# Finishing a batch between the sums of the next: the last feed-forward of a two-layer decoder

## The chip, the cores and the metric

The kernel runs on one core of one Trainium2 chip. A core has a matmul engine (TensorE, PE in the profile, its weight loads PEld), a vector engine (VectorE, DVE), an activation engine (ScalarE, ACT), a general engine (GpSimd, POOL) and a queue for transfers (SyncE, SP). Each engine works through its own list of instructions in order and waits on semaphores for the others. The metric is device time in microseconds (us) of one execution.

## The reference, cut to what matters

The reference is a decoder of two layers with layer norms behind each of six stages, on x of shape 4 x 512 x 512 (four batches of 512 rows). Only the last stage is touched, the second feed-forward with weights packed to four bits:

```python
def _L1_ffn_ref(x, gate_up_packed, gate_up_scales, down_packed, down_scales):
    ...
    w_gu = _dequant_fp4(gate_up_packed, gate_up_scales, GROUP_SIZE)
    w_down = _dequant_fp4(down_packed, down_scales, GROUP_SIZE)
    gate_up = jnp.einsum('bsh,oh->bso', x, w_gu)
    gate, up = (gate_up[..., :I], gate_up[..., I:])
    h = jax.nn.silu(gate) * up
    y = jnp.einsum('bsi,hi->bsh', h, w_down)
    rms = jnp.sqrt(jnp.mean(y * y, axis=-1, keepdims=True) + EPS)
    return y / rms
...
x = _layernorm(x + _L1_ffn_ref(x, ...), axis=-1)
```

I is 1408 and a group of scales spans 128 inputs, so each output of the first product is a sum of four groups, each with a scale of its own.

## The kernel before, in words

The six stages are named A to F, and each runs batch by batch (A0 to A3, and so on to F0 to F3). Each batch of a stage is a Python generator; the function `lanes` keeps at most two alive and steps them in turn. A generator that says "next" lets the following batch begin, so the end of one batch is traced between the steps of the next one. A scheduling layer (Tile) then puts every engine's instructions in order. It keeps the program's dependences and hands out buffers; `tc.issue_after(ins)` adds an edge that puts the instructions of its block behind `ins` on the same engine. Within a generator a `Pipe` delays work by steps: `pipe.later(n, fn)` calls `fn` at the n-th `tick` from now.

The stage in question is `l1_ffn(b)`, F0 to F3. A batch has 11 units (128 of the 1408 inner columns each), a unit has two halves u (0 is gate, 1 is up) and each half four groups g. This makes 88 groups a batch, one a step:

- Two matmuls of 128x512 (L1106, `fg<-fxh,gu` and `fg<-fxl,gu`) fill one PSUM bank with the group's product. A step later `scaled` multiplies by the group's scale and adds. Group 0 of each half is copied by ScalarE (L1064), group 3 of the gate too (L1067); the five others of the unit are sums on VectorE (L1070, `fg<-fg,gs,fg`), 220 in all. GpSimd adds the gate's two parts (L1074).
- ScalarE applies silu (L1078), VectorE multiplies by up (L1082), ScalarE rounds the product to a high part (L1087) and GpSimd takes the low part (L1088).
- `down` multiplies the unit's result into four accumulators, one for each tile of 128 rows: three matmuls for each (L1097, `facc<-...`), spread over eight steps, so twelve a unit. An accumulator holds a PSUM bank from the batch's first unit to its last use.

PSUM has eight banks: four hold a batch's accumulators, and the others pass the groups' products on.

When the eleventh unit's `down` is through, the batch is finished: ScalarE squares each accumulator and sums it along the row (L1116, four times). VectorE takes the mean (L1119, fm), its reciprocal root in eleven small operations (L162, L163 and three times L170 to L172, all 128x4), adds accumulator times root to the residual x for each of the four tiles (L1123) and takes the statistics of the layer norm (L176, L177). A second reciprocal root follows (L185, then again L162 to L172, on ln), the four tiles are normed (L200) and stored. While that goes on for batch b, the groups of batch b+1 are already running on all engines. I call this stretch a handover; there are three (F0 to F1, F1 to F2, F2 to F3). Batch F3 is finished alone.

At the start of a batch, x is transposed by TensorE (L213, `fx<-ident,x`, 16 transposes).

Of the kernel before, what the change touches and what calls it, by code (L numbers as in the profile page):

```python
# [2 lines left out]

# [1 line left out]

# [9 lines left out]
I32 = mybir.dt.int32  # L15
U8 = mybir.dt.uint8
AF = mybir.ActivationFunctionType
ALU = mybir.AluOpType
# [3 lines left out]
B, S, D = 4, 512, 512  # L22
P = 128
NT = 4
MAGIC = 12582912.0
RSQRT_SEED = float(0x5F3759DF)
# [15 lines left out]
class Pipe:  # L42


    def __init__(self):
        self.todo = []
# [21 lines left out]
class Net:  # L68
    def __init__(self, ctx, tc, args):
        self.tc = tc  # L70
        self.nc = tc.nc
        self.a = args
        self.n = 0
        pool = lambda name, **kw: ctx.enter_context(tc.tile_pool(name=name, **kw))
        self.const = pool("const", bufs=1)
        self.op = pool("op", bufs=O_BUFS)
        self.tp = pool("tp", bufs=T_BUFS)
        self.xp = pool("xp", bufs=X_BUFS)
        self.wp_ = pool("wp", bufs=W_BUFS)
        self.small = pool("small", bufs=4)  # L80
        self.psum = pool("psum", bufs=8, space=PSUM)
        nc = self.nc
        tc.keep_in_program_order(nc.scalar.preload_act_table_set(LOG_EXP))
        self.ident = self.c("ident", [P, P])
        make_identity(nc, self.ident)
        self.ident16 = self.c("ident16", [P, P], BF16)
        nc.vector.tensor_copy(self.ident16, self.ident)
        self.ones = self.c("ones", [P, P])
        nc.gpsimd.memset(self.ones, 1.0)
        scratch = lambda name, shape: nc.dram_tensor(name, shape, F32, kind="Internal").ap()  # L90
        self.had_scratch = scratch("had_scratch", (2, NT, 2048, P))
        self.xd = [args["x"]] + [scratch(f"x{i}", (B, S, D)) for i in range(1, 6)] + [args["out"]]
        self.bg, self.table = {}, None
        self.gu, self.dn = {}, []
        self.pre = {}
        self.w1 = {}
        self.mean, self.scale = {}, {}
        self.tern = {name: {} for name in self.TERNARY}
# [69 lines left out]
    def newton(self, ve, y, t):  # L168
        nc = self.nc
        nc.vector.tensor_tensor(t, y, y, ALU.mult)  # L170
        nc.vector.scalar_tensor_tensor(t, t, -0.5, ve, ALU.mult, ALU.mult)
        nc.vector.scalar_tensor_tensor(y, t, 1.5, y, ALU.add, ALU.mult)  # L172

    def ln_stats(self, y, i, ln):
        nc = self.nc
        nc.vector.bn_stats(ln[:, 8:14], y)  # L176
        nc.vector.bn_aggr(ln[:, 2 * i : 2 * i + 2], ln[:, 8:14])  # L177

    def ln_tile(self):
        return self.s("ln", 32, 3)  # L180
# [867 lines left out]
    def l1_ffn(self, b):  # L1048
        nc = self.nc
        pipe = Pipe()  # L1050
        x = self.load_x(5, b)
        yield
        yield
        xT = []
        yield from self.feature_major(pipe, x, "fx", xT)
        yield from pipe.drain()
        acc, y, hs = [], {}, {}

        def scaled(i, u, g, ps):

            s = self.gs[:, (i * 2 + u) * 4 + g : (i * 2 + u) * 4 + g + 1]
            if g == 0:
                y[u] = self.t("fg")
                nc.scalar.activation(y[u], ps, AF.Copy, scale=s)  # L1064
            elif g == 3 and u == 0:
                y2 = self.t("fg2")
                nc.scalar.activation(y2, ps, AF.Copy, scale=s)  # L1067
                y[u, 2] = y2
            else:
                nc.vector.scalar_tensor_tensor(y[u], ps, s, y[u], ALU.mult, ALU.add)  # L1070
            if g == 3:
                o = y.pop(u)
                if (u, 2) in y:
                    nc.gpsimd.tensor_tensor(o, o, y.pop((u, 2)), ALU.add)  # L1074
                pipe.later(F_ACT, *((up, i, o) if u else (gate, o)))

        def gate(o):
            nc.scalar.activation(o, o, AF.Silu)  # L1078
            y["gate"] = o

        def up(i, o):
            nc.vector.tensor_tensor(o, o, y.pop("gate"), ALU.mult)  # L1082
            pipe.later(F_PAIR, pair, i, o)

        def pair(i, o):
            hi, lo = self.t("fhh", F32R), self.t("fhl", F32R)
            nc.scalar.copy(hi, o)  # L1087
            nc.gpsimd.tensor_tensor(lo, o, hi.bitcast(F32), ALU.subtract)  # L1088
            for t in range(NT):
                pipe.later(F_DOWN + 2 * t, down, i, t, (hi, lo))  # L1090

        def down(i, t, h):
            if len(acc) <= t:
                acc.append(self.pb("facc"))
            c = slice(t * P, (t + 1) * P)
            for n, (l, r) in enumerate(((0, 0), (0, 1), (1, 0))):
                nc.tensor.matmul(acc[t], h[l][:, c], self.dn[i][r], start=i == 0 and n == 0, stop=i == 10 and n == 2)  # L1097

        for i in range(11):
            self.need("F", lambda: len(self.dn) > min(10, i + 1))  # L1100
            for u in range(2):
                for g in range(4):
                    pipe.tick()
                    ps = self.pa("fg")
                    for n in range(2):
                        nc.tensor.matmul(ps, self.gu[i, u][:, g * P : (g + 1) * P], xT[g][n], start=n == 0, stop=n == 1)  # L1106
                    pipe.later(F_SCALED, scaled, i, u, g, ps)
                    yield
        yield "next"
        x = self.load_x(5, b)  # L1110
        yield from pipe.drain()
        fm = self.s("fm", 24, 2)
        ss, ve = fm[:, 0:4], fm[:, 4:8]
        for i in range(NT):
            sq = self.t("fsq")
            nc.scalar.activation(sq, acc[i], AF.Square, accum_out=ss[:, i : i + 1])  # L1116
            if i % 2:
                yield
        nc.vector.tensor_scalar(ve, ss, 1.0 / 512.0, 1e-6, ALU.mult, ALU.add)  # L1119
        r = self.rsqrt(ve, fm[:, 8:20])  # L1120
        ln = self.ln_tile()
        for i in range(NT):
            nc.vector.scalar_tensor_tensor(x[i], acc[i], r[:, i : i + 1], x[i], ALU.mult, ALU.add)  # L1123
            self.ln_stats(x[i], i, ln)
            if i % 2:
                yield
        self.finish(pipe, x, ln, 5, b)
        yield from pipe.drain()
# [124 lines left out]
```

## Time and profile before

| | us |
|---|---|
| median of three runs (1626.9 to 1636.79) | 1629.89 |
| the profiled execution, its own time | 1630.29 |
| its span, first to last instruction | 1628.6 |

| engine | busy us | share of the span | instructions |
|---|---|---|---|
| PE | 1532.3 | 94% | 8215 |
| DVE | 1247.6 | 77% | 2684 |
| ACT | 1010.6 | 62% | 2177 |
| POOL | 665.9 | 41% | 672 |

| line, engine, what | count | busy us | mean ns |
|---|---|---|---|
| L1070 DVE, sums of the groups | 220 | 162.4 | 745 |
| L1106 PE, `fg<-fxh,gu` | 352 | 143.7 | 408 |
| L1106 PE, `fg<-fxl,gu` | 352 | 138.8 | 394 |
| L1074 POOL, adding the gate's parts | 44 | 61.1 | 1388 |
| L1064 ACT, copies of group 0 | 88 | 60.4 | 686 |
| L1097 PE, `facc<-p4h,fhh` (one of three) | 176 | 71.2 | 406 |

A row of the timeline or of a group gives start and duration, engine, line, operation and `out<-in`; what stands in brackets is the idle time of the engine before it and what ended that. A busy PE isn't PE at its peak, since the ends of matmuls are modelled and overlap: the distance between the starts of matmuls says more. In rows by stretch, x is the number of instructions, and PEclk the clock that TensorE was granted, as a share of full speed. Stage F takes the last 350 us, from the first L1106 at 1280.0 us on.

### The profile page before, as it was taken

What the parts mean: (1) busy time and instruction counts of PE and PEld (TensorE: products, weight loads), DVE (VectorE), ACT (ScalarE), POOL (GpSimd) and SP (SyncE); (2) the same over time, 40 slices, a digit from 0 to 9 for tenths busy, and PEclk for the clock granted to TensorE, in tenths of its full rate; (3) what the DMA queues carried; (4) which work ended last, traced back from release to release, by engine and by line L of the source; (5) the groups of instructions that cost most, each with busy time, mean ns of one, the idle gap of its engine ahead of it and who ended that gap; (6) DMA issues with size and microseconds to landing.
All of it is one profiled execution on the core that took longest, in us unless ns stands there. A gap on an engine that the chain in (4) does not pass through costs nothing.

```text
span 1628.6 us, 25543 instructions
## 1 busy us (share of the span) xinstructions
PE 1532.3 (94%) x8215; PEld 1100.0 (68%) x8246; DVE 1247.6 (77%) x2684; ACT 1010.6 (62%) x2177; POOL 665.9 (41%) x672
## 2 busy tenths in 40 slices
PE   7999999999999999899999999999998889999995
PEld 5888786444544664476777767777676766687774
DVE  6476589999875788977575766657779898979795
ACT  4333336988777887787796756967543445454542
POOL 6663563555535204422334243342333244333332
PEclk9999999999999999999999999999999999999998
DMA  7143344455124734861523334232446331111000
GB/s 241 35 149 123 110 149 137 146 172 174 59 75 132 222 116 136 250 188 61 145 60 77 79 90 117 60 86 68 155 155 196 128 113 53 43 37 52 1 26 26
DMA packets 127812, 180.76 MB, mean 111 GB/s; under 512 B 16560, under 2 KB 51376, under 8 KB 127680
## 3 DMA queue, kind: packets, MB, share of 16 engines
q1 hardware_dynamic: 123552, 170.69, 33.7%
q0 software_dynamic: 4128, 8.46, 2.1%
q8 instruction: 65, 1.06, 0.3%
q14 instruction: 67, 0.55, 0.1%
HBM read 111.98 MB, written 41.94 MB: 95 GB/s over the span
## 4 chain that ended last, share of the span: by engine, by line
PE 61%; DVE 17%; ACT 9%; issue 5%; DMA 4%; POOL 3%; SPq 1%; DVEq 0%; ACTq 0%; POOLq 0%
PE fg L1106 7%; PE facc L1097 6%; PE dT L883 3%; PE bo L458 2%; ACT de L873 2%; PE dn L701 2%; PE bT L213 2%; DVE x L200 2%; PE pu L649 2%; PE bs L486 2%; DVE bsm L434 2%; PE pg L647 2%; PE do L903 2%; DVE fg L1070 2%; PE dq L150 2%
## 5 line engine op out<-in xcount | busy, mean ns | idle before, releaser
L1070 DVE SCALAR_TENSOR_TENSOR fg<-fg,gs,fg 128x512 f32<-128x512 f32 x220 | 162.4, 745 | 35.4 <-PE fg L1106 15.2
L869 DVE CUSTOM_DVE_ANT_0 de<-ds,negm,thr 128x128 f32<-128x128 f32 (+3 forms) x256 | 126.4, 546 | 34.3 <-PE ds L858 31.2
L1106 PE MATMUL fg<-fxh,gu 128*128 128x512 f32 x352 | 143.7, 408 | 8.0 <-DVE fg L1070 5.0
L873 ACT ACTIVATE de<-de,dm 128x128 f32<-128x128 f32 (+3 forms) x256 | 143.1, 563 | 12.4 <-DVE dm L869 11.9
L1106 PE MATMUL fg<-fxl,gu 128*128 128x512 f32 x352 | 138.8, 394 | 0.0
L442 POOL TENSOR_SCALAR be<-be,bsm 128x512 f32<-128x512 f32 x128 | 95.8, 761 | 104.5 <-DVE bsm L440 72.8
L624 POOL TENSOR_TENSOR hl<-g,hh 128x512 fp32r<-128x512 f32 x64 | 83.9, 1318 | 113.3 <-ACT hh L623 98.7
L1074 POOL TENSOR_TENSOR fg<-fg,fg 128x512 f32<-128x512 f32 x44 | 61.1, 1388 | 127.1 <-ACT fg L1067 74.5
L436 ACT ACTIVATE be<-bs,bsm 128x512 f32<-128x512 f32 x128 | 87.3, 690 | 31.3 <-DVE bsm L434 29.6
L800 POOL TENSOR_TENSOR dql<-dqf,dqh 128x512 fp32r<-128x512 f32 x32 | 41.3, 1290 | 155.3 <-ACT dqh L799 121.0
L883 PE MATMUL dT<-ident,de 128*128 128x128 f32 x640 | 89.6, 278 | 7.6 <-ACT de L873 5.8
L1106 PEld LDWEIGHTS fg<-fxh,gu 128*128 128x128 f32 x352 | 66.9, 190 | 38.4 <-DVE fg L1070 14.8
L883 PEld LDWEIGHTS dT<-ident,de 128*128 128x128 f32 x640 | 71.7, 141 | 25.3 <-ACT de L873 13.6
L1064 ACT ACTIVATE fg<-fg,gs 128x512 f32<-128x512 f32 x88 | 60.4, 686 | 39.2 <-PE fg L1106 38.6
L434 DVE TENSOR_REDUCE bsm<-bs 128x1 f32<-128x512 f32 x128 | 83.3, 672 | 0.0
L1097 PE MATMUL facc<-p4h,fhh 128*128 128x512 f32 x176 | 71.2, 406 | 8.9 <-DVE fg L1070 6.2
L458 PE MATMUL bo<-bpT,cT 128*64 128x512 f32 x256 | 76.9, 618 | 2.1 <-ACT bpT L449 1.2
L213 PEld LDWEIGHTS bT<-ident,be 128*128 128x128 f32 x512 | 55.0, 141 | 34.6 <-issue 10.3
L213 PE MATMUL bT<-ident,be 128*128 128x128 f32 x512 | 73.2, 281 | 4.4 <-POOL be L442 2.1
L1067 ACT ACTIVATE fg<-fg,gs 128x512 f32<-128x512 f32 x44 | 30.3, 688 | 73.4 <-PE fg L1106 73.4
L312 POOL TENSOR_TENSOR z<-z,rope_cos 128x512 f32<-128x512 f32 x32 | 45.7, 1438 | 73.0 <-DVE zs L310 66.0
L1106 PEld LDWEIGHTS fg<-fxl,gu 128*128 128x128 f32 x352 | 66.8, 190 | 11.9
(332 smaller groups left out, 4693.3 us busy)
## 6 DMA issues: line engine op xcount, KB each, us to landing
x<-x SPq DMA_DIRECT2D x176, 256.0 KB, 3.1
had_scratch<-hw SPq DMA_DIRECT2D x64, 256.0 KB, 2.4
z<-had_scratch SPq DMA_DIRECT2D x64, 256.0 KB, 5.8
stk<-dqh SPq DMA_DIRECT2D x192, 64.0 KB, 2.0
tw<-in_wg_t SPq DMA_DIRECT2D x32, 256.0 KB, 3.8
tw<-in_wu_t SPq DMA_DIRECT2D x32, 256.0 KB, 3.6
tw<-in_wd_t SPq DMA_DIRECT2D x32, 256.0 KB, 2.9
p<-in_gu_p SPq DMA_DIRECT2D x22, 256.0 KB, 2.7
```

What stands on the lines that cost most here:

```text
L213: self.nc.tensor.transpose(pt[:, i * P : (i + 1) * P], srcs[i][:, j * P : (j + 1) * P], self.ident)
L434: nc.vector.tensor_reduce(sm[:, h : h + 1], ps, AX.X, ALU.max, negate=True)
L436: nc.scalar.activation(e, ps, AF.Exp, bias=sm[:, h : h + 1], accum_out=sm[:, 2 + h : 3 + h])
L442: nc.gpsimd.tensor_scalar(es[h][i], es[h][i], sm[:, 4 + h : 5 + h], 1.0, ALU.mult, ALU.mult)
L458: nc.tensor.matmul(po[0][h * 64 : h * 64 + 64, :], cT[j][:, c : c + 64], pTs[h], start=j == 0, stop=j == NT - 1)
L624: nc.gpsimd.tensor_tensor(lo, g, hi.bitcast(F32), ALU.subtract)
L869: nc.vector.tensor_tensor_reduce(es[i], ps, self.negm[:, 384 - P * i :], -1.0, self.thr[:, i : i + 1], ALU.add, ALU.min, n4[:, i : i + 1])
L873: nc.scalar.activation(es[i], es[i], AF.Exp, bias=n4[:, i : i + 1], scale=-1.0, accum_out=den[:, hh * 4 + i : hh * 4 + i + 1])
L883: nc.tensor.transpose(pt[:, o + (i - j) * P : o + (i - j + 1) * P], es[i][:, j * P : (j + 1) * P], self.ident)
L1070: nc.vector.scalar_tensor_tensor(y[u], ps, s, y[u], ALU.mult, ALU.add)
L1097: nc.tensor.matmul(acc[t], h[l][:, c], self.dn[i][r], start=i == 0 and n == 0, stop=i == 10 and n == 2)
L1106: nc.tensor.matmul(ps, self.gu[i, u][:, g * P : (g + 1) * P], xT[g][n], start=n == 0, stop=n == 1)
```

## The change

Three things change for batches F0 to F2; the end of F3 stays as it is.

1. As soon as an accumulator has had its last matmul (`i == 10`), one step later, ScalarE copies it from PSUM to SBUF (`release`, a tile `fy` from the large pool), and all that follows reads the copy. The bank is free after the copy.
2. The squares on ScalarE and all of the finish on VectorE are cut into pieces, and `between` issues each piece alone: it waits for a step (up to four while the piece before is not yet followed by a sum), and puts the piece behind the engine's latest group operation (`self.emitted`) by an edge. `ahead` then puts the engine's next group operation behind the piece by another edge. The pieces on VectorE are: the mean; the root's first two operations; three times a Newton step of three operations; for each tile its L1123 and then its statistics; the variance plus epsilon; the second root in the same four pieces; four norms, each followed by its store.
3. `newton` and `ln_stats` return their last instruction, and the tile `ln` is taken earlier.

```diff
+    def between(self, engine, *ops):
+
+        yield
+        for _ in range(3):
+            if engine in self.piece:
+                yield
+        with self.tc.issue_after(self.emitted[engine].ins):
+            for op in ops:
+                self.piece[engine] = op()
+
+    def ahead(self, engine):
+
+        p = self.piece.pop(engine, None)
+        return self.tc.issue_after(p.ins) if p else nullcontext()
+
+    def rsqrt_spread(self, ve, s):
+
+        nc = self.nc
+        sh, y, t = s[:, 0:4], s[:, 4:8], s[:, 8:12]
+        yield from self.between(
+            "DVE",
+            lambda: nc.vector.tensor_scalar(sh.bitcast(I32), ve.bitcast(I32), 1, None, ALU.logical_shift_right),
+            lambda: nc.vector.tensor_scalar(y.bitcast(I32), sh.bitcast(I32), -1.0, RSQRT_SEED, ALU.mult, ALU.add),
+        )
+        for _ in range(3):
+            yield from self.between("DVE", lambda: self.newton(ve, y, t))
+        return y
...
             else:
-                nc.vector.scalar_tensor_tensor(y[u], ps, s, y[u], ALU.mult, ALU.add)
+                with self.ahead("DVE"):
+                    self.emitted["DVE"] = nc.vector.scalar_tensor_tensor(y[u], ps, s, y[u], ALU.mult, ALU.add)
...
+            if i == 10 and b + 1 < B:
+                pipe.later(1, release, t)
+
+        def release(t):
+
+            f = self.o("fy")
+            nc.scalar.copy(f, acc[t])
+            acc[t] = f
...
+        if b + 1 < B:
+            for i in range(NT):
+                sq = self.t("fsq")
+                yield
+                yield from self.between("ACT", lambda: nc.scalar.activation(sq, acc[i], AF.Square, accum_out=ss[:, i : i + 1]))
+            yield
+            yield from self.between("DVE", lambda: nc.vector.tensor_scalar(ve, ss, 1.0 / 512.0, 1e-6, ALU.mult, ALU.add))
+            r = yield from self.rsqrt_spread(ve, fm[:, 8:20])
+            for i in range(NT):
+                yield from self.between("DVE", lambda: nc.vector.scalar_tensor_tensor(x[i], acc[i], r[:, i : i + 1], x[i], ALU.mult, ALU.add))
+                yield from self.between("DVE", lambda: self.ln_stats(x[i], i, ln))
+            v2 = ln[:, 16:20]
+            yield from self.between("DVE", lambda: nc.vector.tensor_scalar(v2, ln[:, 0:8].rearrange("p (i two) -> p i two", two=2)[:, :, 1], 1e-5, None, ALU.add))
+            yield from self.rsqrt_spread(v2, ln[:, 20:32])
+            for i in range(NT):
+                yield from self.between("DVE", lambda: nc.vector.tensor_scalar(x[i], x[i], ln[:, 2 * i : 2 * i + 1], ln[:, 24 + i : 25 + i], ALU.subtract, ALU.mult))
+                nc.sync.dma_start(self.xd[6][b, i * P : (i + 1) * P, :], x[i])
+            return
```

The two copies on ScalarE in `scaled` (L1064 and L1067) are wrapped in `ahead("ACT")` and kept in `self.emitted["ACT"]` in the same way.

More of the change, by code (lines that the diff above doesn't have):

```diff
@@ L1 @@
 import math
-from contextlib import ExitStack
+from contextlib import ExitStack, nullcontext
 import numpy as np
@@ L92, in __init__ @@
         self.xd = [args["x"]] + [scratch(f"x{i}", (B, S, D)) for i in range(1, 6)] + [args["out"]]
-        self.bg, self.table = {}, None
+        self.bg, self.table, self.emitted, self.piece = {}, None, {}, {}
         self.gu, self.dn = {}, []
@@ L171, in newton @@
         nc.vector.scalar_tensor_tensor(t, t, -0.5, ve, ALU.mult, ALU.mult)
-        nc.vector.scalar_tensor_tensor(y, t, 1.5, y, ALU.add, ALU.mult)
+        return nc.vector.scalar_tensor_tensor(y, t, 1.5, y, ALU.add, ALU.mult)
+    def between(self, engine, *ops):
[20 more added lines that the diff above has]
+        return y
     def ln_stats(self, y, i, ln):
@@ L176, in ln_stats @@
         nc.vector.bn_stats(ln[:, 8:14], y)
-        nc.vector.bn_aggr(ln[:, 2 * i : 2 * i + 2], ln[:, 8:14])
+        return nc.vector.bn_aggr(ln[:, 2 * i : 2 * i + 2], ln[:, 8:14])
     def ln_tile(self):
@@ L1063, in scaled @@
                 y[u] = self.t("fg")
-                nc.scalar.activation(y[u], ps, AF.Copy, scale=s)
+                with self.ahead("ACT"):
+                    self.emitted["ACT"] = nc.scalar.activation(y[u], ps, AF.Copy, scale=s)
             elif g == 3 and u == 0:
                 y2 = self.t("fg2")
-                nc.scalar.activation(y2, ps, AF.Copy, scale=s)
+                with self.ahead("ACT"):
+                    self.emitted["ACT"] = nc.scalar.activation(y2, ps, AF.Copy, scale=s)
                 y[u, 2] = y2
             else:
-                nc.vector.scalar_tensor_tensor(y[u], ps, s, y[u], ALU.mult, ALU.add)
+                with self.ahead("DVE"):
+                    self.emitted["DVE"] = nc.vector.scalar_tensor_tensor(y[u], ps, s, y[u], ALU.mult, ALU.add)
             if g == 3:
@@ L1113, in l1_ffn @@
         ss, ve = fm[:, 0:4], fm[:, 4:8]
+        ln = self.ln_tile()
+        if b + 1 < B:
[16 more added lines that the diff above has]
+            return
         for i in range(NT):
@@ L1120, in l1_ffn @@
         r = self.rsqrt(ve, fm[:, 8:20])
-        ln = self.ln_tile()
         for i in range(NT):
```

## The prediction

> **What bounds the kernel now.** I read the page first, then busy time by stretch over the last feed-forward (1280 us to the end), then the timeline of VectorE, GpSimd and TensorE through one handover of a batch, and the chain of waits there. The change touches only this stage: in the built order of both kernels every engine's instructions are the same until batch F0 has finished its matmuls.
>
> Busy time by stretch, batch F1 handing over to F2 and the quiet part after it:
>
> ```profile
> core 0: us, PE busy (x) PEld busy (x) DVE busy (x) ACT busy (x) POOL busy (x), PEclk, DMA share, GB/s
> 1440.00:1460.00 20.00, 20.00 (x98) 16.68 (x97) 14.05 (x20) 9.93 (x16) 5.14 (x4) 1.00 0.16 53
> 1460.00:1480.00 20.00, 17.96 (x70) 13.61 (x69) 17.40 (x35) 10.02 (x21) 7.70 (x6) 0.91 0.00 0
> 1480.00:1500.00 20.00, 18.95 (x80) 14.11 (x79) 19.56 (x38) 10.03 (x16) 8.47 (x6) 1.00 0.08 28
> 1500.00:1520.00 20.00, 20.00 (x89) 16.54 (x89) 15.60 (x22) 9.29 (x15) 8.07 (x7) 1.00 0.23 79
> ```
>
> Outside the handover TensorE is the limit: 89 matmuls in 20 us, VectorE busy 15.6. In the handover it starts only 70 and 80, and VectorE is full (19.56 of 20). The timeline of VectorE and GpSimd there shows why it is so full:
>
> ```profile
> 1465.86 0.16 DVE L1119 TENSOR_SCALAR fm<-fm 128x4 f32<-128x4 f32 x1
> 1466.05 0.17 DVE L162 TENSOR_SCALAR fm<-fm 128x4 int32<-128x4 int32 x1
> 1466.11 1.30 POOL L1074 TENSOR_TENSOR fg<-fg,fg 128x512 f32<-128x512 f32 x1 [3.10 <-DVE fm L1119]
> 1466.26 1.18 DVE L163 TENSOR_SCALAR fm<-fm 128x4 int32<-128x4 int32 x1
> ...
> 1467.37 1.27 POOL L1088 TENSOR_TENSOR fhl<-fg,fhh 128x512 fp32r<-128x512 f32 x1
> ...
> 1467.47 1.18 DVE L170 TENSOR_TENSOR fm<-fm 128x4 f32<-128x4 f32 x1
> 1468.69 0.16 DVE L171 SCALAR_TENSOR_TENSOR fm<-fm 128x4 f32<-128x4 f32 x1
> 1468.77 0.75 DVE L1070 SCALAR_TENSOR_TENSOR fg<-fg,gs,fg 128x512 f32<-128x512 f32 x1
> 1469.44 0.15 DVE L172 SCALAR_TENSOR_TENSOR fm<-fm 128x4 f32<-128x4 f32 x1
> 1469.57 0.50 PE L1097 MATMUL facc<-p4h,fhh 128*128 128x512 f32 x1 [1.92 <-DVE fg L1070]
> ```
>
> A 128x4 operation of 0.17 us takes 1.18 us twice: each time it ends within 0.03 us of the end of a GpSimd operation (1467.41, 1468.64). I call that a port wait. The sums (L1070), which read PSUM, never show it (220 of them, at most 0.754 us). Meanwhile TensorE stands still for 1.92 us for want of a sum. The chain of waits at the end of the same handover:
>
> ```profile
> 1496.19 2.88 DVE x L200 x4
> 1499.07 0.67 DVE fg L1070
> 1499.74 0.04 issue
> 1499.79 1.20 PE fg L1106 x4
> ```
>
> The four norms stand in one lump ahead of a sum that TensorE waits for. So in the handover VectorE is the bound, and the banks between it and TensorE are its only slack.
>
> **What a handover costs now.** In the TensorE timeline the first transposes (L213) of F2 start at 1446.36, those of F3 at 1524.86: a period of 78.5 us. Its work is 176 matmuls of L1106 and 132 of L1097; forty in a row start in 9.07 us (1454.74 to 1463.81), 0.2268 us each, so 69.9 us, and 16 transposes at some 0.1 us make 71.5. Lost: 7.0 us. F2 to F3 repeats it to 0.1 us. F0 to F1 has the same stalls, but without the slow matmuls (0.43 us apart from 1470.4 to 1473.4, clock 0.91): 1 us less, 6.0. All three: 20.0 us, the most that this change can bring.
>
> **VectorE's account before.** From the first of the chain (1465.86) to the first sum behind the norms (1499.0) are 33.1 us, of which 1.0 idle (0.73 and 0.30) and 6.1 port waits, each an operation's time less its undisturbed time (1.01, 1.01, 1.09, 1.01, 0.55, 0.50 and 0.97 in the norms). Ten GpSimd operations fall into it: 0.61 us of wait for each. In this stretch TensorE passes 103 matmuls, 23.4 us at its pace. Excess 33.1 - 23.4 = 9.7 us; 7.0 were lost, so the banks swallowed 2.7.
>
> **The change, part by part.**
>
> *The pieces move.* In the built order the first piece came after the sum of group 106 (groups of two L1106 matmuls, numbered from F0's first; eight a unit), in the run of nine groups (104 to 112) that have no L1097 matmuls between them, where VectorE (five sums and a product, 4.3 us) is slower than TensorE (eight groups, 3.6 us) even without pieces. Now it comes after group 117, and one piece stands between any two sums until group 151. TensorE's share of that stretch is 119 matmuls, 27.0 us, against 23.4: this is the gain.
>
> *VectorE's work in it.* 22 sums at 0.67 us (start to start, 1468.77 to 1469.44) are 14.7; four products L1082 at 0.58, 2.3; 24 small operations, 14 at 0.19 and 10 (the last ahead of a sum) at 0.08, 3.5; four L1123 at 0.65, four L176 at 0.60, four L177 at 0.13, 5.5; four norms at 0.45 (L200 takes 0.525 at least, less overlap), 1.8. Together 27.8 us.
>
> *Port waits.* GpSimd's work goes by units: two operations a unit, 34 groups are 4.25 units, so 8.5 operations at 0.61, 5.2 us. New is that L1123 (L1163 after the change) reads fy from SBUF, not facc from PSUM. No row shows it; the nearest is L1082, two SBUF inputs, median 0.683 and at most 1.151 (it waits), against L1123 with PSUM, 0.717 to 0.751 (it never does). GpSimd is busy 41% of the time, the rest of an operation is 0.65 us on average: 0.27 each, 1.1 for four. I take 6.3 us. Ends: none (0) and every GpSimd operation hitting for its whole 1.30 us (11.1).
>
> The Trainium skill's page "SBUF — State Buffer", section "Who interferes with whom", speaks against this edit: a VectorE instruction with two SBUF inputs contends with a GpSimd instruction that reads SBUF, and whichever came second stands still for the whole of the other. The rows above agree for L170 and L1082. With all four caught at their whole length, the rule's worst, they would cost 5.2 us and not 1.1, 4.1 more a handover, and the sum would be 1635.8 us.
>
> *Sum of a handover.* 27.8 + 6.3 - 27.0 = 7.1 us of excess, less the same 2.7 of slack: 4.4 us lost. Gain 2.6 in F1 to F2 and F2 to F3, 1.6 in F0 to F1: 6.8 us.
>
> *ScalarE's copies.* Twelve of 128x512 out of PSUM (four a handover, the last batch has none); the nearest row is the cast L139 fxh<-fx, 0.59 us, so 2.4 us a handover. ScalarE is busy 10.0 of 20 us in both stretches and takes them in its gaps. Uncovered, each would push the L1064 copy queued behind it, and with it a bank, by up to 0.59 us; that is within the slack of four banks. In return the four accumulator banks are free some 14 us sooner (about 1464 against 1477.8), so the run of nine groups finds eight banks. The copies and the SBUF source leave L1116 at its 0.59 us.
>
> *Edges.* The squares stand between ScalarE's copies now, the fourth after group 115; VectorE's first piece, after group 117, comes 1.6 us of TensorE's time later, about when the square is done: at most 0.3 us. Behind it stands the sum of group 118. No instruction is added on VectorE or GpSimd, none removed. On SP the last store of a batch falls behind one x load; no one waits for the store. F3's own ending is as before, so a gain in any handover reaches the end whole.
>
> The Trainium skill's page "TensorE: Matmul & The Clock Gate", section "What's actually happening", has the slow clock come after an idle window of about 3.4 us. Here the 0.43 us cadence follows a standstill of 1.92 us, and at 1390.2 an equal standstill has none behind it. By the page no slow clock should be there to remove; by the trace it is 1 us in two handovers of three, inside the measured 7.0. By the page the gain would be 2 us smaller, 1625.5 us.
>
> **The sum.** The profiled execution took 1630.3 us (span 1628.6), 0.4 over the median of 1629.9. 1630.3 - 6.8 = 1623.5 us.
>
> **Rivals.**
> 1. *The forecast*, a small gain: port waits of 4 to 9 us a handover. At 4 the loss is 2.1, gains 4.9, 4.9 and 3.9, 1616.6 us; at 9 the loss is 7.1, 1631.6 us. Chance 0.74.
> 2. *All is hidden.* With port waits under 2 us nothing is lost and all 20.0 us come back: 1610.3 us. For it: VectorE has 9 us idle in the quiet 1425 to 1457. Against: ten GpSimd operations in a handover, seven of which hit. Chance 0.11.
> 3. *Slower by the port.* Pieces between all sums, and L1123 with two SBUF inputs, let nearly every GpSimd operation stop VectorE. From port waits of 8.9 us on (where the loss passes 7.0) the change loses; at 11.1 and 1 us idle the loss is 10.2, and 3.2 + 3.2 + 4.2 make 1640.9 us. For it: an alternation of 0.67 us sums with short all-SBUF pieces leaves no gap as long as 1.3 us. Against: the same alternation stood in the chain of 1486 to 1495, with 0.5 to 1.0 us a hit. Chance 0.15.
>
> **How the numbers follow.** The measurement tells about 1% (16.3 us) from no change; the three runs before lie 9.9 us apart. Most of the forecast is inside 1%, and so is nearly all of the third case; only the second, and a little of the first, go past 1613.6. Faster by over 1%: 0.11; within: 0.87; slower by over 1%: 0.02. The range runs from between the first and second cases to just past port waits of 9 us: 1613 to 1634.
>
> **What would show it.** Right: the period of F2 to F3 (first transposes to first transposes) falls from 78.5 to some 76 us; the 1.92 us standstill and the clock of 0.91 are gone; no lump of four norms in the chain; port waits of 4 to 9 us a handover, some now in L1163; VectorE still full between groups 117 and 151. Wrong: the period at 72 (port waits vanished, or more slack than 2.7 us), or over 78.5 (waits above 9 us, or a piece that waits for ScalarE's fourth square).

## The result, and the profile after

The change makes the kernel slower by a quarter of a per cent: 1635.06 us against 1630.39, medians of 22 runs each, ratio 1.0025 (95% interval 1.0014 to 1.0035). The forecast was 1623.5 us.

The profiled execution has a span of 1634.7 us, 6.1 more than before. Part of that is not the change: up to the first sum of F0 the two programs are the same, and this execution is 2.5 us later there (1287.4 against 1284.9). From there on it loses 3.7 us, all of it in the three columns that hold a handover. I measure from the first sum (L1070, L1101 after the change) of one batch to that of the next:

| us between first sums | F0 to F1 | F1 to F2 | F2 to F3 | first sum of F3 to the end |
|---|---|---|---|---|
| before | 89.5 | 77.2 | 78.5 | 98.4 |
| after | 89.5 | 78.6 | 79.3 | 100.0 |

The handover of F0 to F1 lies behind the first sum of F1 and so in the second column, that of F1 to F2 in the third, that of F2 to F3 in the last. The third column is called the period below.

Busy time by stretch, kernel after, F1 handing over to F2 (columns as in the prediction's table of stretches):

```profile
1460.00:1480.00 20.00, 20.00 (x89) 16.40 (x88) 15.96 (x26) 14.29 (x28) 7.78 (x6) 1.00 0.00 0
1480.00:1500.00 20.00, 16.77 (x71) 12.62 (x70) 19.04 (x39) 7.96 (x13) 6.24 (x5) 1.00 0.00 1
1500.00:1520.00 20.00, 17.65 (x76) 13.49 (x75) 16.52 (x30) 7.74 (x13) 7.28 (x6) 1.00 0.32 105
```

The first of the three was 70 matmuls before and is now full (89): the pieces are out of the run of nine groups, and the standstill of 1.92 us at its end is gone. But the next two start 71 and 76, and in the last VectorE is busy only 16.5 of 20 us. TensorE waits there for something that isn't VectorE's work. The chain of waits names it (start, duration, engine, tile, line):

```profile
1489.32 0.25 DVE fg L1113
...
1490.02 0.62 ACT fhh L1118
...
1490.77 1.69 POOL fhl L1119
1492.46 1.24 POOL fg L1105
1493.70 0.02 issue
1493.72 0.63 ACT fg L1109
1494.35 0.59 ACT fg L1093
1494.93 0.04 issue
1494.98 0.73 PE fg L1145 x2
```

A product on VectorE (L1113) is late. ScalarE's cast of it (L1118) waits; GpSimd's low part (L1119) waits for the cast; GpSimd's add (L1105), of the *next* unit, whose last input (a sum) was there at 1490.64, stands behind the low part until 1492.42; the silu (L1109) waits for that add; ScalarE's copy of the next group 0 (L1093) stands behind the silu; and TensorE has no bank until it is done. (The low part takes 1.69 us where most take 1.30. It starts while a sum into x, L1163, is running on VectorE; I take the 0.39 us for a port wait in the other direction, which is argued.) ScalarE's timeline of the same time, with the idle time before each in brackets:

```profile
1490.00 0.62 ACT L1118 CAST fhh<-fg 128x512 fp32r<-128x512 f32 x1 [0.75 <-DVE ln L205]
1493.72 0.63 ACT L1109 ACTIVATE fg<-fg 128x512 f32<-128x512 f32 x1 [3.09 <-POOL fg L1105]
1494.26 0.67 ACT L1093 ACTIVATE fg<-fg,gs 128x512 f32<-128x512 f32 x1
1496.91 0.69 ACT L1097 ACTIVATE fg<-fg,gs 128x512 f32<-128x512 f32 x1 [1.98 <-PE fg L1145]
1497.89 0.69 ACT L1093 ACTIVATE fg<-fg,gs 128x512 f32<-128x512 f32 x1 [0.29 <-PE fg L1145]
1498.47 0.61 ACT L1118 CAST fhh<-fg 128x512 fp32r<-128x512 f32 x1
```

The chain comes once a unit (the next two adds stand 2.8 and 1.6 us behind their last input), and from the second time on it feeds itself: the next product is ready at 1496.09, but its cast starts only at 1498.47, behind ScalarE's copies (L1097, L1093), which had waited for the delayed TensorE. Standstills of TensorE behind the copy end at 1495.0, 1503.1 and 1511.0 (2.6, 1.3 and 1.8 us from start to start, where 0.23 is usual; together 5.1 us beyond that, of which a little may be matmuls missing from the trace). One more, of 1.4 us, ends at 1486.0 with a late sum. F0 to F1 has the same four to 0.3 us. The waits of this handover, longest in total, show the same pairs:

```profile
POOL fhl L1119 <- ACT fhh L1118: 21.9, 5, 6.0
...
ACT fg L1109 <- POOL fg L1105: 10.5, 4, 3.1
PEld fg L1145 <- ACT fg L1093: 6.5, 5, 2.7
```

Before the change the last of these pairs took 0.7 us there, and GpSimd waited 6.6 us for the cast. What made the chain is in the built order, which was at hand before the result. ScalarE's instructions over groups 116 to 144 (units 14 to 18, counted from F0's first), g the copies by group, "cast" L1087 or L1118 and "silu" L1078 or L1109:

```
before    g116 cast silu g120 g123 g124 silu cast g128 g131 g132 cast g136 silu g139 g140 silu cast g144
after     g116 cast silu g120 g123 g124 cast silu g128 g131 g132 cast silu g136 g139 g140 cast silu g144
```

Before, the silu mostly stood ahead of the cast, or the copy between them; after, the cast is always first. GpSimd has the low part ahead of the next unit's add in four units of each handover (16 to 19, 27 to 30, 38 to 41); before the change only in the first of each four, and the add is ahead in the others. Why it came out so is argued, not shown: the built order of TensorE is quite regular in this stretch (two groups, then an accumulator's three matmuls), as if VectorE kept up, and with a punctual VectorE the cast's product is there in time.

### The profile page after: what moved, and what is told of

Its sections match the earlier page's. It is cut to its first block, busy times and chain, and to the rows that moved or that the text cites. A ratio compares the mean times of both kernels' runs of the same rounds, so it can differ in the third digit from the quotient of the medians.

```text
span 1634.7 us, 25547 instructions
## 1 busy us (share of the span) xinstructions
PE 1531.3 (94%) x8215; PEld 1100.6 (67%) x8246; DVE 1244.7 (76%) x2684; ACT 1016.4 (62%) x2189; POOL 666.1 (41%) x672
## 5 line engine op out<-in xcount | busy, mean ns | idle before, releaser
L1101 DVE SCALAR_TENSOR_TENSOR fg<-fg,gs,fg 128x512 f32<-128x512 f32 x220 | 162.8, 744 | 37.9 <-ACT fg L1093 17.5
L1105 POOL TENSOR_TENSOR fg<-fg,fg 128x512 f32<-128x512 f32 x44 | 58.8, 1337 | 87.4 <-ACT fg L1097 44.3
L1119 POOL TENSOR_TENSOR fhl<-fg,fhh 128x512 fp32r<-128x512 f32 x44 | 59.1, 1343 | 85.8 <-ACT fhh L1118 78.8
L1093 ACT ACTIVATE fg<-fg,gs 128x512 f32<-128x512 f32 x88 | 60.1, 683 | 23.5 <-PE fg L1145 23.5
```

The lines of the kernel that those rows point to most:

```text
L1101: self.emitted["DVE"] = nc.vector.scalar_tensor_tensor(y[u], ps, s, y[u], ALU.mult, ALU.add)
```

## The experiments

**Theory 1.** VectorE's lag, which the change only moves, travels over cast, low part, add and silu to the group-0 copy, because of the order on ScalarE and GpSimd. **Theory 2.** VectorE's work and port waits between the sums are the loss. **Theory 3.** ScalarE's copies, and the sums that now read two SBUF operands, are the loss.

**The cast two steps later (pair5).** This turns the order on ScalarE and GpSimd and, from F1 on, leaves TensorE's and VectorE's lists as they are (in F0 both come out in another order).

```diff
-F_SCALED, F_ACT, F_PAIR, F_DOWN = 1, 5, 3, 9
+F_SCALED, F_ACT, F_PAIR, F_DOWN = 1, 5, 5, 7
```

Built, ScalarE reads `g116 silu g120 cast g123 g124 silu g128 cast g131`, and GpSimd has the add first in all twelve units named above.

> The changed kernel with the delays F_PAIR 3 to 5 and F_DOWN 9 to 7: the built order of TensorE and VectorE stays the same instruction for instruction; on ScalarE the cast of the high part now stands behind the next silu and the next group-0 copy, on GpSimd the add ahead of the low part. Theory 1 (VectorE's lag travels over cast, low part, add and silu to the group-0 copy, whose bank TensorE waits for): the period from F2's first sum to F3's first sum falls from 79.3 us to 75.5 to 76.5, the time to about 1626 us, 0.995 to 0.998 of the kernel before. Theory 2 (VectorE's own work and port waits between groups 117 and 151 set the loss): period 79.0 to 79.6, ratio 1.0025. Theory 3 (ScalarE's twelve copies and the second SBUF operand): also no change, 79.3.

Measured: 1626.07 us, ratio 0.9979 (0.9969 to 0.9989), period 75.8 us. The period fell by 3.5 us. TensorE's standstills behind ScalarE's copy fell from 5.1 to 2.2 us beyond the usual pace. Theory 3 had nothing to change here. Theory 2 isn't quite out of it: with GpSimd's operations in another place the port waits fell as well, from 5.4 to 4.0 us, so that up to 1.4 of the 3.5 us may be theirs. Busy time by stretch of this kernel, the same part of the handover:

```profile
1460.00:1480.00 20.00, 19.99 (x88) 16.25 (x88) 15.89 (x29) 15.22 (x30) 8.13 (x6) 1.00 0.00 0
1480.00:1500.00 20.00, 18.42 (x78) 13.94 (x78) 19.66 (x42) 7.79 (x13) 7.48 (x6) 1.00 0.00 1
1500.00:1520.00 20.00, 19.13 (x84) 15.25 (x83) 17.21 (x27) 9.18 (x15) 7.81 (x7) 1.00 0.32 106
```

78 and 84 matmuls against 71 and 76, and VectorE full again where TensorE falls behind. VectorE goes through the same 21 sums and all pieces in 31.3 us without idling; after the change it took 33.5, of which 0.7 idle. The first column rose from 89.5 to 93.4 us: the delay also reaches F0, where VectorE still unpacks weights and its list changes too.

**The longer delay without the other order (pair4).** Delays 4 and 8. The cast still comes ahead of silu and copy from group 120 on.

```diff
-F_SCALED, F_ACT, F_PAIR, F_DOWN = 1, 5, 3, 9
+F_SCALED, F_ACT, F_PAIR, F_DOWN = 1, 5, 4, 8
```

> The changed kernel with delays 4 and 8 in place of 3 and 9: the cast is traced one step later, but from group 120 on the built order of ScalarE and GpSimd is that of the change (cast ahead of silu and group-0 copy, low part ahead of the add). Theory 1 (it is the order, not the delay): period 78.3 to 79.5 us. Rival (the longer delay itself helps, by the time that the product has): 77.5 us or less.

Measured once: 1633.82 us, period 80.4 us, and 79.2 in the second column. The period is 0.9 above the range that I gave, in the direction away from the rival. The slow clock explains it: in this execution seven matmuls from 1493.4 on stand 0.43 us apart (clock 0.91 from 1480 to 1500), which is 1.4 us that the change didn't have in this handover. GpSimd has the low part first in the same units as after the change. So one step of delay without the other order gains nothing; the second step was not tried without it.

**The same delay in the kernel before (before_pair5).** The edit is that of pair5, on the kernel before.

> The kernel before with the same two delays (F_PAIR 5, F_DOWN 7). Theory 1: there the silu mostly stood ahead of the cast already, so little is to be had: period 77.5 to 78.5 us, ratio 0.998 to 1.000. Theory 2 and 3: no change, 78.5 us, unless the lumps of pieces fall elsewhere.

Measured: 1636.82 us, ratio 1.0046 (1.0029 to 1.0062), period 79.5 us. A miss: I had expected a small gain. 3.8 us of it are F0's, as above (93.3). The other 1 to 2 us a handover I put down to pieces that fall in a worse place: nine small operations (the mean and eight of the first root) now stand in one lump ahead of a sum. VectorE's timeline:

```profile
1471.98 0.16 DVE L1119 TENSOR_SCALAR fm<-fm 128x4 f32<-128x4 f32 x1
1472.17 1.25 DVE L162 TENSOR_SCALAR fm<-fm 128x4 int32<-128x4 int32 x1
1473.46 1.19 DVE L163 TENSOR_SCALAR fm<-fm 128x4 int32<-128x4 int32 x1
...
1475.76 0.75 DVE L1070 SCALAR_TENSOR_TENSOR fg<-fg,gs,fg 128x512 f32<-128x512 f32 x1
```

3.8 us without a sum, where it was 2.9 before, and TensorE stands still behind it (2.57 us), with the slow clock after, now in all three handovers where it was in two. The delay is no gain by itself; it gained only with the pieces spread.

**Copies alone (copies_only).** The edit turns the new branch off (`if b + 1 < B:` becomes `if False:`), so the old finish runs on the copies.

> The changed kernel with ScalarE's copies, but with the finish as it was before the change (reading the copies, in lumps, without edges). Theory 1: the order on ScalarE is mostly silu ahead of cast again, and the banks are free sooner: period 77 to 78.5 us, ratio 0.998 to 1.000. Theory 3 (copies and the second SBUF operand cost): 79 us or more, ratio 1.002 or more.

Measured: 1626.67 us, ratio 0.9986 (0.9975 to 0.9998), period 77.4 us. Theory 3 falls: the copies don't cost. They gain 1.1 us in the handovers F1 to F2 and F2 to F3 and nothing in F0 to F1 (77.2 in the second column, as before). That is where the slow clock was: before the change seven matmuls stand 0.43 us apart in each of the two handovers, 1.4 us, and in this kernel there are none; so the gain goes with the slow clock. The longest standstill that VectorE causes here is 1.47 us, not 1.92. Two of the sums into x do wait for GpSimd in this kernel: two together took 2.44 us where two took 1.41 out of PSUM, and one took 1.34.

**No finish at all (no_finish).** The edit replaces squares, roots, sums and norms of F0 to F2 by four stores of the copies.

> The changed kernel without the finish of F0 to F2: squares, roots, sums and norms are left out, the copied accumulators are stored. The order on ScalarE and GpSimd stays that of the change (cast ahead of silu). Theory 1 (the order costs only together with a lag of VectorE): period 71.5 to 72.5 us, no standstill. A rival, that the order alone makes TensorE wait: 74 us or more.

Measured once: 1609.8 us, period 71.6 us, all matmuls at their pace. Only half of the order is that of the change, other than I expected. ScalarE has the cast ahead of the silu throughout, but GpSimd has the add ahead of the low part in the units that matter, as in pair5:

```profile
1404.67 1.29 POOL L1105 TENSOR_TENSOR fg<-fg,fg 128x512 f32<-128x512 f32 x1 [3.38 <-ACT fg L1097]
1405.92 1.30 POOL L1119 TENSOR_TENSOR fhl<-fg,fhh 128x512 fp32r<-128x512 f32 x1
```

So the cast ahead of the silu costs nothing by itself while VectorE is on time; what only the change and pair4 have, in four units of each handover, is GpSimd's half of the order. Whether GpSimd's order would cost without a lag of VectorE, this run doesn't show. In the change the fourth add of the handover starts 2.4 us behind its last input (1516.08) and no standstill follows. The run also measures the floor: F1 to F2 lost 78.5 - 71.6 = 6.9 us before (1.4 of it the slow clock) and 7.6 after, 4.2 with the later cast. The prediction's second rival, with all hidden, had put the floor at 1610.3 us.

**The later cast only where it is needed (hand).**

```diff
-            pipe.later(F_PAIR, pair, i, o)
+            late = 2 if b and i < 8 else 0
+            pipe.later(F_PAIR + late, pair, i, o)
...
-                pipe.later(F_DOWN + 2 * t, down, i, t, (hi, lo))
+                late = 2 if b and i < 8 else 0
+                pipe.later(F_DOWN - late + 2 * t, down, i, t, (hi, lo))
```

> The changed kernel with the later cast (two steps) only for the first eight units of F1 to F3, so that F0, which took 3.8 us longer with the delay everywhere, keeps its old order. Theory 1: the handovers as with the delay everywhere, period F2 to F3 75.6 to 76.2 us, the F0 period back at 89.5; time 1621 to 1623 us, ratio 0.995 to 0.996. If the gain of the later cast had come from anything but the handovers: period above 77 us.

Measured: 1622.84 us, ratio 0.9958 (0.9942 to 0.9974), period 75.8 us, the first column back at 89.5.

**Without GpSimd's low part (no_low).** pair5 with `hi = lo = self.t("fhh", F32R)` and no L1119; the low part is left out of the third matmul.

> The changed kernel with the later cast everywhere, and without GpSimd's low part (the third matmul of each accumulator reads the high part again): half of GpSimd's operations are gone from stage F. The account of port waits: 4.3 us a handover become some 2.2, and the period falls from 75.8 to 73.5 to 74.5 us. Rival (the loss left is VectorE's own work, the waits fall into its slack): 75.3 us or more.

Measured once: 1610.95 us, period 73.9 us; port waits 2.2 us in the handover of F1 to F2 against 4.0 in pair5 (4.3 in the expectation). So of the 4.2 us that a handover still loses, 1.9 go with half of GpSimd's operations, about as much as the port waits fell. This speaks for theory 2 in what is left, without proving it: the edit also takes an instruction out of the chain of theory 1. And VectorE's lag still travels in pair5: two of the three standstills of that handover (1.4 and 1.3 us from start to start) end with the group-0 copy, behind a silu that waited for GpSimd's add. (The first column fell too, by 7.8 us against pair5, so its whole time isn't to be set against the handovers.)

**Norms on ScalarE (hand_norm_act).** hand, and

```diff
+            nm = fm[:, 20:24]
+            mean = ln[:, 0:8].rearrange("p (i two) -> p i two", two=2)[:, :, 0]
+            yield from self.between("DVE", lambda: nc.vector.scalar_tensor_tensor(nm, mean, -1.0, ln[:, 24:28], ALU.mult, ALU.mult))
+            yield
             for i in range(NT):
+                yield
-                yield from self.between("DVE", lambda: nc.vector.tensor_scalar(x[i], x[i], ln[:, 2 * i : 2 * i + 1], ln[:, 24 + i : 25 + i], ALU.subtract, ALU.mult))
+                yield from self.between("ACT", lambda: nc.scalar.activation(x[i], x[i], AF.Identity, bias=nm[:, i : i + 1], scale=ln[:, 24 + i : 25 + i]))
```

> The same, with the four norms of each handover on ScalarE (scale and bias from the second root, one more small operation on VectorE). VectorE is the bound of what is left (4.2 us a handover): four norms of 0.45 us and their port waits of 0.3 us less one small operation are 1.9 us less of its work, of which some comes through: period 74 to 75.2 us, ratio 0.992 to 0.995. Rival: ScalarE's copy of group 0 is what TensorE waits for, and four more operations ahead of it cost: 76 us or more.

Measured: 1618.31 us, ratio 0.9930 (0.9914 to 0.9947), period 74.6 us. This is the fastest whole kernel, 0.7% under the one before.

What wasn't tried: the order on GpSimd turned alone, with the cast left in its place; and the spread without the copies. There the accumulators would stay in PSUM until late pieces read them while the next batch's four need banks, and I expect that the lists as ordered would wait for each other.

## Why the prediction was wrong

*VectorE's account held.* It put the stretch from the first piece to the first sum behind the norms at 27.8 + 6.3 = 34.1 us (with 22 sums; there are 21). In F1 to F2 it took 33.5, with 5.4 of port waits (1.05 in the mean, 0.98 in a Newton step, 0.62 in the sums into x, 2.13 in the second root, 0.63 in the norms) and 0.7 idle. TensorE's share, 119 matmuls, was 27.0 as said.

*The new SBUF operand was a small term, as sized.* The forecast gave it 1.1 us for the four; 0.62 in F1 to F2. The row of the changed kernel, its sums into x out of fy:

```profile
L1163 DVE SCALAR_TENSOR_TENSOR x<-fy,fm,x x12: 741/822/1200, 1404.8 to 1572.6; 128x512 f32<-128x512 f32 x12
```

Minimum, median and maximum in ns: out of PSUM they were 717, 738 and 751. So the sum does wait for GpSimd now, up to 0.46 us: the six long ones (0.90 and 1.20 us) all end 0.55 us behind the end of a GpSimd operation. This is in agreement with the Trainium skill (page "SBUF — State Buffer", section "Who interferes with whom"), by which two SBUF inputs contend with a GpSimd instruction that reads SBUF. The worst by that rule, 4.1 us more a handover, did not come; that its 1635.8 us lies next to the measured 1635.06 is chance.

*The step that failed is "less the same 2.7 of slack".* The forecast took four banks as the only thing between VectorE and TensorE, and carried the slack of the old order into the new one. In the new order VectorE's lag reaches TensorE through five instructions on two other engines, 0.62 + 1.69 + 1.24 + 0.63 + 0.59 = 4.8 us after the product, and the slack is gone: excess 33.5 - 27.0 = 6.5, loss 7.6, which is 1.1 more than the excess. With the cast behind the copy the loss is 4.2, and hand with its 1622.84 us comes next to the forecast's 4.4 and 1623.5. That is luck: VectorE's stretch is 31.3 us there and not 34.1, the excess 4.3, so the slack is 0.1 and not 2.7, and the two errors cancel. In copies_only, with the finish in lumps, 2.5 us of slack are left (31.7 - 23.4 - 5.8). So the spread itself takes the slack, and the order of the change makes it negative. Why the slack is gone even in the better order stays open; the shorter chain that is left there, add, silu and copy, is a candidate.

*The same step stands behind the sentences on ScalarE.* The copies did go into its gaps (14.3 of 20 us busy, no standstill in that stretch), and in copies_only, with the finish in lumps, they cost nothing. But "each would push the L1064 copy queued behind it" was said of the copies alone. That the change reorders what was there already, on engines with time to spare, was not asked, though the built order showed it.

*Rival 3* had the sign, but not its mechanism: port waits were 5.4 us, well under its 8.9. (By the prediction's own sum the three handovers together break even at 8.6, since F0 to F1 had only 6.0 to lose.) Of its other mishap, a piece that waits for ScalarE's fourth square, nothing was seen.

*The signs named beforehand.* The standstill of 1.92 us and the lump of norms went, as said. Port waits were in the range of 4 to 9 us, some of them in L1163. The period was to be 76 us and was 79.3, past the 78.5 named as a sign of being wrong, but for neither of the two reasons named with it; VectorE wasn't full throughout (16.5 of 20 us in the last stretch); and the slow clock, which was to go, stayed in F2 to F3 (0.91 from 1560 to 1580), behind one of the new standstills.

## What to carry to other kernels

When a change spreads work over a busy engine, list what the *other* engines' orders become, and follow each in-order list from the late engine to whatever the bound engine waits for: an engine with time to spare still sets the pace when an instruction whose input is late stands ahead of one that the bound engine waits for. Here turning the order on two such engines, with two steps of delay on one cast, was worth 3.5 us a handover and turned a loss into a gain. And read the order of every engine in the experiments too: no_finish was built to keep the order of the change and kept it on one engine only.

## What the runs showed of the hardware that was not expected

- The slow clock of TensorE didn't follow from the length of a standstill alone. In the kernel after, the standstill of 2.22 us that ends at 1494.98 has full speed behind it (0.23 us from start to start); an equal one that ends at 1574.25 in the same execution is followed, from 1.5 us later, by matmuls 0.43 us apart:

```profile
1574.25 0.50 PE L1145 MATMUL fg<-fxh,gu 128*128 128x512 f32 x1 [2.22 <-ACT fg L1093]
...
1575.77 0.63 PE L1145 MATMUL fg<-fxl,gu 128*128 128x512 f32 x1
1576.19 0.63 PE L1128 MATMUL facc<-p4h,fhh 128*128 128x512 f32 x1
```

- ScalarE's square takes 0.623 us out of SBUF (median of 12) where it took 0.597 out of PSUM (median of 16).
